# Node tiles in pairs, degrees per two groups, and gates applied in the tail of a graph and expert kernel

## The chip, the core and the metric

The kernel runs on one core of a Trainium2 chip, as one launch. The metric is the time on the device in microseconds. TensorE does the matrix products and transposes (PE in the profile, its weight loads PEld), VectorE (DVE) and ScalarE (ACT) the elementwise work, GpSimd (POOL) issues the indirect DMAs, which gather or scatter rows by a list of indices, and SyncE (SP) issues plain DMAs. Each engine works through its own instructions in order and waits on semaphores for the others.

## The reference

There are 12500 nodes with 256 features, 212500 edges sorted by their destination, and 64 experts with a hidden width of 512, of which each node uses two. Cut to what matters:

```python
def _forward(feats, ...):                      # feats is x, 12500 x 256
    deg_out = clip(segment_sum(ones, src), 1.0)
    deg_in = clip(segment_sum(ones, dst), 1.0)
    h = feats * rsqrt(deg_out)[:, None]
    m = segment_sum(h[src], dst) * rsqrt(deg_in)[:, None]
    x = m @ W_gc + b_gc + (feats @ W_res + b_res)
    core = moe(x)
    y = x + core
    mean, var = over the nodes, for each feature
    return (y - mean) * rsqrt(var + 1e-5) * gamma + beta

def moe(x):
    logits = x @ Wg + bg
    vals, idx = top_k(logits, 2)
    gates = softmax(vals)                      # of the two
    # expert e: gelu(x @ w1[e] + b1[e]) @ w2[e] + b2[e], for its first 1024 places
    return the sum over the two of gate * expert(x)

out = layernorm(x + _forward(x, ...))          # over the features
```

The softmax of two logits is a pair of gates: with d = second minus first, exp(d) is taken, the first gate is 1 / (1 + exp(d)) and the second exp(d) / (1 + exp(d)).

## The kernel before

Nodes are cut into 98 tiles of 128 (the last has 84), edges into 1664 columns of 128, and the columns into 208 groups of 8. Since the edges are sorted, the destinations of one group fall into a window of 128 nodes. The kernel has a setup (degrees by `src`, group windows, `h` scaled and written to `h_d`) and three stages.

**Node stage.** The loop over the groups calls `sums(g, n0, t0)`, and as soon as a node tile has all its edges, `node(t)`: once every two groups, now and then after three, twice after the last. In `sums`, each of the eight columns has an indirect DMA by POOL (L493) that gathers 128 rows of `h_d` into one of 16 tiles of `ring`, a one-hot matrix `o` made by VectorE (L499), and a matmul into `p` (L500), which has a last column of ones, so it counts the edges as well. `p` is copied by ScalarE to `s` (L503), transposed into `q` (L510), and VectorE adds it to the accumulator `acc2` in SBUF at the window's first node `n0` (L513). The counts go through `e` (L507), which splits them over the two node tiles that a window can touch, and a small matmul with `shift` (L511) into the last two columns of `q`, and are added to `deg_in` at a column `t0` read at run time (L515). `n0` and `t0` come in registers that VectorE loads for four groups at a time, eight values.

`node(t)` takes the reciprocal root of the in-degrees (`rsqrt`, L166 to L172: a root on ScalarE, four small operations and a reciprocal on VectorE), loads and scales the node's own features `xt` (L527), transposes them into `tp` (L530), copies them to `xT` (L532), and multiplies accumulator and features by the weights into `gp` (L535, L539; 256 features and 64 logits). VectorE scales and adds the bias: `y` (L540) and the logits `lg` (L549). Then come the two best experts (`top`, `i8`), the gates (exp on ScalarE L558, three VectorE operations to L561, kept in two extra columns of `y`), the store of `y` to `x2_d` by SP (L564), the rank of each token in its expert (`both` L572, matmuls into a part of `tp` L576 and L577, `ahead` L579, `total` L580, `junk` L584), the place code (L591 to L604), and four matmuls into the tables `tab` (L609 to L620). `tp` and `gp` have one buffer each, most other tiles of the node two. The exp and the root belong to different function tables, so ScalarE changes tables twice in a node.

**Experts.** After the tables are complete, the experts run in an order of their load. `gather` fetches rows of `x2_d` by POOL (L736), 258 floats a row: features and the two gate columns. `turn` transposes them (L752, copy L756) and picks the gate of each row (L758), `hidden` and `outputs` do the two matrix products (L770, L786). `outputs` adds the bias (L791), scales by the gate on ScalarE (L792), and scatters the rows to `z_d` by POOL (L793), which holds one row for each of a node's two choices. SP loads the weights.

**Tail.** For loads of eight node tiles, SP brings both rows of every node (`zt`, two buffers, L900), VectorE adds them to `acc2`, which by then holds `x`, in four additions (L904), TensorE transposes the sum (L915), and VectorE takes batchnorm statistics (L919). After the batchnorm numbers, a second loop applies them, adds the input and does the layernorm (L965 to L999).

The framework orders each engine's instructions so that node work is spread between the groups that follow; the source order above is not the engine's order.

Of the kernel before, what the change touches and what calls it, by code (L numbers as in the profile page):

```python
# [7 lines left out]
F32 = mybir.dt.float32  # L8
# [10 lines left out]
P = 128  # L19
# [3 lines left out]
E = 64  # L23
# [36 lines left out]


# [17 lines left out]
def gnn_moe_kernel(  # L79
# [25 lines left out]
    x2_d = dram.tile([N, D + 2], F32, name="x2_d")  # L105
# [53 lines left out]
    deg_in = const.tile([P, NT + 1], F32)  # L159
    V.memset(deg_in, 0.0)  # L160

# [29 lines left out]
    tables = route.tile([P, 2, 3, NSLOT], I32)  # L191
# [18 lines left out]
    til = edge.tile([P, NG, 2], F32)  # L210
    n0_row = edge.tile([1, 2, NG], I32)
# [4 lines left out]
    with ExitStack() as stack:  # L216
# [49 lines left out]
        def windows():  # L266
# [9 lines left out]
            V.tensor_copy(n0_row[:, 0], n0[:, 0])  # L276
            V.tensor_single_scalar(n0_row[:, 1], n0_row[:, 0], 7, op=ALU.arith_shift_right)
            V.tensor_copy(n0[:, 1], n0_row[:, 1])
# [34 lines left out]
            V.tensor_sub(til[:, :, 1], dig[:, 1], n0_b[:, 1])  # L313
            V.tensor_scalar(til[:, :, 0], til[:, :, 1], -1.0, 1.0, op0=ALU.mult, op1=ALU.add)
# [150 lines left out]
    with ExitStack() as stack:  # L465
# [21 lines left out]
        def sums(g, n0, t0):  # L487
# [14 lines left out]
            s = two.tile([P, D], F32, name="s")  # L502
            S.copy(s, p[:, :D])  # L503
            shift = two.tile([P, P], F32, name="shift")
            V.tensor_scalar(shift, lane, low[:, g : g + 1], None, op0=ALU.is_equal)
            e = two.tile([P, 2], F32, name="e")
            V.tensor_scalar(e, til[:, g], p[:, D:], None, op0=ALU.mult)  # L507
            q = ps2.tile([P, 2 * P + 2], F32, name="q")
            for h in range(2):
                T.transpose(q[:, h * P : (h + 1) * P], s[:, h * P : (h + 1) * P], ident)  # L510
            T.matmul(q[:, 2 * P :], shift, e, start=True, stop=True)  # L511
            m = acc2[:, :, bass.ds(n0, W)]
            V.tensor_add(m, q[:, : 2 * P].rearrange("p (h n) -> p h n", h=2), m)  # L513
            m = deg_in[:, bass.ds(t0, 2)]
            V.tensor_add(m, q[:, 2 * P :], m)  # L515

        def node(t):
            r = rows(t)
            y = two.tile([P, D + 2], F32, name="y")
            d_in = two.tile([P, 1], F32, name="d_in")  # L520
            V.tensor_scalar_max(d_in, deg_in[:, t : t + 1], 1.0)
            rsqrt(two, r_in[:, t : t + 1], d_in)
            root = two.tile([P, 1], F32, name="root")
            V.tensor_mul(root, d_in, r_in[:, t : t + 1])
            xt = two.tile([P, D], F32, name="xt", bufs=3)
            S.dma_start(xt[:r], x[t * P : t * P + r])
            S.activation(xt[:r], xt[:r], AF.Copy, scale=root[:r])  # L527
            tp = ps1.tile([P, 3, P], F32, name="tp")
            for k in range(2):
                T.transpose(tp[:, k, :r], xt[:r, k * P : (k + 1) * P], ident[:r, :r])  # L530
            xT = two.tile([P, 2, P], F32, name="xT")
            S.copy(xT[:, :, :r], tp[:, :2, :r])  # L532
            gp = ps1.tile([P, DL], F32, name="gp")
            for k in range(2):
                T.matmul(  # L535
                    gp[:r], acc2[:, k, t * P : t * P + r], wcat[:, k], start=k == 0, stop=False
                )
            for k in range(2):
                T.matmul(gp[:r], xT[:, k, :r], wcat[:, 2 + k], start=False, stop=k == 1)  # L539
            V.scalar_tensor_tensor(  # L540
                y[:r, :D], gp[:r, :D], r_in[:r, t : t + 1], bias[:r, :D],
                op0=ALU.mult, op1=ALU.add,
            )
            S.copy(
                acc2[:r, :, t * P : t * P + P],
                y[:r, :D].rearrange("p (h d) -> p h d", h=2),
            )
            lg = two.tile([P, E], F32, name="lg")
            V.scalar_tensor_tensor(  # L549
                lg[:r], gp[:r, D:], r_in[:r, t : t + 1], bias[:r, D:], op0=ALU.mult, op1=ALU.add  # L550
            )
            top = two.tile([P, 8], F32, name="top")
            V.max(top[:r], lg[:r])
            i8 = two.tile([P, 8], U32, name="i8")
            V.max_index(i8[:r], top[:r], lg[:r])
            e2 = two.tile([P, 2], F32, name="e2")
            V.tensor_sub(e2[:r, 0:1], top[:r, 1:2], top[:r, 0:1])
            S.activation(e2[:r, 0:1], e2[:r, 0:1], AF.Exp)  # L558
            V.tensor_scalar_add(e2[:r, 1:2], e2[:r, 0:1], 1.0)
            V.reciprocal(y[:r, D : D + 1], e2[:r, 1:2])  # L560
            V.scalar_tensor_tensor(  # L561
                y[:r, D + 1 :], e2[:r, 0:1], -1.0, y[:r, D : D + 1], op0=ALU.add, op1=ALU.mult
            )
            nc.sync.dma_start(x2_d[t * P : t * P + r], y[:r])  # L564
            ix = two.tile([P, 2], F32, name="ix")
            V.tensor_copy(ix[:r], i8[:r, 0:2])


            o1 = two.tile([P, E], BF16, name="o1")
            V.tensor_scalar(o1[:r], lane_b[:r, :E], ix[:r, 0:1], None, op0=ALU.is_equal)  # L570
            both = two.tile([P, E], BF16, name="both")
            V.scalar_tensor_tensor(  # L572
                both[:r], lane_b[:r, :E], ix[:r, 1:2], o1[:r], op0=ALU.is_equal, op1=ALU.add
            )
            pp = tp[:, 2].rearrange("p (k e) -> p k e", e=E)
            T.matmul(pp[:r, 0], before[:r, :r], both[:r], start=True, stop=True)  # L576
            T.matmul(pp[:, 1], ones_b[:r], both[:r], start=True, stop=True)  # L577
            ahead = two.tile([P, E], F32, name="ahead")
            V.tensor_add(ahead[:r], pp[:r, 0], total[:r])  # L579
            V.tensor_add(total, pp[:, 1], total)  # L580
            junk = two.tile([P, E], F32, name="junk")
            rk = two.tile([P, 2], F32, name="rk")
            for k in range(2):
                V.scalar_tensor_tensor(  # L584
                    junk[:r], lane[:r, :E], ix[:r, k : k + 1], ahead[:r],
                    op0=ALU.is_equal, op1=ALU.mult, accum_out=rk[:r, k : k + 1],
                )


            rk_i = two.tile([P, 2], I32, name="rk_i")  # L590
            V.tensor_copy(rk_i[:r], rk[:r])  # L591
            V.tensor_single_scalar(rk_i[:r], rk_i[:r], 7, op=ALU.arith_shift_right)
            blk = two.tile([P, 2], F32, name="blk")
            V.tensor_copy(blk[:r], rk_i[:r])
            lo = two.tile([P, 2], F32, name="lo")
            V.scalar_tensor_tensor(
                lo[:r], blk[:r], float(-P), rk[:r], op0=ALU.mult, op1=ALU.add
            )
# [28 lines left out]
        for g in range(NG):  # L627
# [19 lines left out]
            while done < ready:  # L647
                node(done)
                done += 1
# [391 lines left out]
```

## Time and profile before

| | us |
|---|---|
| median of 3 runs | 3864.94 |
| lowest, highest | 3864.89, 3868.7 |
| profiled execution, its time | 3846.16 |
| profiled execution, its span | 3844.4 |
| busy in the span: PE, PEld | 2581.5, 1896.3 |
| busy in the span: DVE, ACT, POOL | 1689.2, 1047.0, 2067.6 |
| first gather of the node stage, last | 247.9, 2687.4 |
| first expert gather | about 2729 |

The mean granted clock of TensorE is 0.806 of full speed. The profiled execution is one run and stands 18.8 us below the median; all durations of rows come from it. A line of the profile names source line, engine, operation, written and read tiles, and how often; "idle before" is how long the engine had waited, with the instruction that released it. A busy share over the whole span says little here, since the stages have different limits: the span is read by stage.

### The profile page before, as it was taken

To read this page: it belongs to the slowest core of one execution; us is meant where nothing else is said; L and a number is where in the kernel's file an instruction comes from. 1 tells how busy PE (TensorE), PEld (TensorE's weight loads), DVE (VectorE), ACT (ScalarE), POOL (GpSimd) and SP (SyncE) were. 2 spreads that over 40 slices of the span, in tenths; PEclk is the share of its full clock that TensorE was granted. 3 is DMA by queue.
4 is the path that set the end of the run, shared out by engine and by line. 5 is a ranking of instruction groups with operands and counts; after the bars stand their busy time and mean duration, and the time that the engine had idled before them with its cause. 6 is when DMAs were issued, how large, how long until landed. Compare 5 with 4: busy or idle time off the path is not lost. (4 is left out here: it accounts for less than half of the span.)

```text
span 3844.4 us, 40947 instructions
## 1 busy us (share of the span) xinstructions
PE 2581.5 (67%) x11395; PEld 1896.3 (49%) x11395; DVE 1689.2 (44%) x7659; ACT 1047.0 (27%) x2367; POOL 2067.6 (54%) x2165
## 2 busy tenths in 40 slices
PE   6725476565656656656665665665699999999630
PEld 5614354444444544444444444444477776777620
DVE  9953254443444444434444444444422222222497
ACT  8901021121112121212121122121233333333218
POOL 0046666666666666666666666666355555555100
PEclk8857788777778777777778677777899999999755
DMA  5085543333333333333333333333334444566666
GB/s 170 2 282 189 165 110 102 102 101 100 102 100 101 101 103 97 99 103 99 99 99 101 99 98 102 100 99 97 101 114 119 139 134 153 171 184 192 221 201 201
DMA packets 245787, 485.64 MB, mean 126 GB/s; under 512 B 45047, under 2 KB 157341, under 8 KB 237362
## 3 DMA queue, kind: packets, MB, share of 16 engines
q0 software_dynamic: 102640, 275.69, 25.6%
q1 hardware_dynamic: 128848, 194.48, 15.7%
q10 hardware_dynamic: 14066, 12.81, 1.1%
q8 instruction: 92, 1.51, 0.2%
q14 instruction: 141, 1.16, 0.1%
HBM read 393.01 MB, written 93.22 MB: 126 GB/s over the span
## 5 line engine op out<-in xcount | busy, mean ns | idle before, releaser
L493 POOL DMA_INDIRECT ring<-h_d,src_col x1664 | 1579.3, 949 | 873.4 <-issue 358.6
L500 PE MATMUL p<-ring,o 128*128 128x257 f32 x3328 | 994.8, 441 | 70.8 <-DMA z_d<-zero 51.0
L500 PEld LDWEIGHTS p<-ring,o 128*128 128x128 f32 x3328 | 702.3, 223 | 205.0 <-issue 90.6
L499 DVE TENSOR_SCALAR o<-lane,rel 128x128 f32<-128x128 f32 x1664 | 423.7, 301 | 193.3 <-remote 112.2
L786 PE MATMUL yp<-w,h 128*128 128x256 f32 (+3 forms) x1928 | 434.8, 381 | 4.1 <-ACT h L774 4.1
L770 PE MATMUL hp<-xT,w 128*128 128x384 f32 (+11 forms) x1328 | 400.2, 455 | 1.3 <-issue 1.3
L736 POOL DMA_INDIRECT xg<-x_d,tables x241 | 232.9, 967 | 305.6 <-PE xtp L752 208.1
L786 PEld LDWEIGHTS yp<-w,h 128*128 128x128 f32 (+3 forms) x1928 | 342.3, 182 | 70.0 <-issue 7.3
L535 PE MATMUL gp<-wcat,acc 128*128 128x320 f32 x392 | 185.5, 609 | 268.1 <-DVE acc L513 173.6
L513 DVE TENSOR_TENSOR acc<-q,acc 128x256 f32 x208 | 88.0, 423 | 564.2 <-remote 373.9
L503 ACT COPY s<-p 128x256 f32<-128x256 f32 x208 | 77.2, 371 | 921.7 <-remote 591.7
L793 POOL DMA_INDIRECT z_d<-yo,tables x241 | 238.0, 987 | 146.5 <-ACT yo L792 80.5
L770 PEld LDWEIGHTS hp<-xT,w 128*128 128x128 f32 x1328 | 248.3, 191 | 132.0 <-issue 59.2
L510 PE MATMUL q<-ident,s 128*128 128x128 f32 x416 | 103.7, 335 | 306.0 <-issue 185.0
L535 PEld LDWEIGHTS gp<-wcat,acc 128*128 128x128 f32 x392 | 94.0, 260 | 325.2 <-DVE acc L513 190.8
L510 PEld LDWEIGHTS q<-ident,s 128*128 128x128 f32 x416 | 62.6, 168 | 357.8 <-issue 215.5
L792 ACT ACTIVATE yo<-yo,gate 128x256 f32<-128x256 f32 (+3 forms) x241 | 122.3, 508 | 393.3 <-DVE yo L791 286.8
L791 DVE TENSOR_TENSOR yo<-yp,bb 128x256 f32<-128x256 f32 (+3 forms) x241 | 102.0, 423 | 284.1 <-PE yp L786 184.6
L774 ACT ACTIVATE h<-hp,w 128x384 f32<-128x384 f32 (+11 forms) x332 | 177.9, 544 | 170.4 <-PE hp L770 148.6
L539 PE MATMUL gp<-wcat,xT 128*128 128x320 f32 x392 | 152.9, 521 | 86.7 <-ACT xT L532 50.0
L756 DVE COPY xT<-xtp 128x768 f32<-128x768 f32 (+2 forms) x83 | 77.4, 932 | 299.8 <-PE xtp L752 299.5
L620 PE MATMUL tab<-at,vals 128*128 128x512 bf16 x392 | 144.4, 502 | 68.1 <-DVE at L609 28.8
(224 smaller groups left out, 3106.5 us busy)
## 6 DMA issues: line engine op xcount, KB each, us to landing
w<-in_wpack SPq DMA_DIRECT2D x64, 1026.0 KB
ring<-h_d,src_col POOLq DMA_INDIRECT x1664
z_d<-zero SPq DMA_DIRECT2D x98, 256.0 KB
zt<-z_d SPq DMA_DIRECT2D x24, 1024.0 KB
x_d<-y SPq DMA_DIRECT2D x97, 129.0 KB
xt<-in_x ACTq DMA_DIRECT2D x97, 128.0 KB
z<-in_x SPq DMA_DIRECT2D x12, 1024.0 KB
out<-z SPq DMA_DIRECT2D x12, 1024.0 KB
```

Of the source, the lines that this page charges most:

```text
L493: GP.indirect_dma_start(out=r[:, :D], out_offset=None, in_=h_d, in_offset=bass.IndirectOffsetOnAxis(ap=src_col[:, c : c + 1], axis=0),)
L499: V.tensor_scalar(o[:, j], lane, rel[:, c : c + 1], None, op0=ALU.is_equal)
L500: T.matmul(p, o[:, j], r, start=j == 0, stop=j == GR - 1)
L510: T.transpose(q[:, h * P : (h + 1) * P], s[:, h * P : (h + 1) * P], ident)
L535: T.matmul(gp[:r], acc2[:, k, t * P : t * P + r], wcat[:, k], start=k == 0, stop=False)
L539: T.matmul(gp[:r], xT[:, k, :r], wcat[:, 2 + k], start=False, stop=k == 1)
L620: T.matmul(tab[i], vals[:r, i], at[:r], start=t == 0 and k == 0, stop=t == NT - 1 and k == 1,)
L736: GP.indirect_dma_start(out=g, out_offset=None, in_=x2_d, in_offset=bass.IndirectOffsetOnAxis(ap=at[:, 0, k : k + 1], axis=0),)
L770: T.matmul(hp[:, :m], w1[:, c, j * P : (j + 1) * P], xT[:, c, :m], start=c == 0, stop=c == 1,)
L774: S.activation(h1[:, j, :m], hp[:, :m], AF.Gelu, bias=w[:, 2 * H + 4 * D + j : 2 * H + 4 * D + j + 1],)
L786: T.matmul(yp[:r], h1[:, j, k * P : k * P + r], w2[:, j], start=j == 0, stop=j == 3,)
L793: st = GP.indirect_dma_start(out=z_d, out_offset=bass.IndirectOffsetOnAxis(ap=at[:r, 1, k : k + 1], axis=0), in_=yo[:r], in_offset=None, b ...
```

## The change

Four things are done together.

1. `node(t)` becomes `nodes(t0, n)` and takes two tiles at once, except the last two tiles, which stay single. The small operations (degrees, roots, places) cover both tiles; transposes, matrix products and one-hot work are done for each tile in turn. `tp` has four parts instead of three, `gp` still one buffer. It is called after every second group only, if both tiles have their edges. The bias operation covers features and logits in one.
2. The degree counts of two groups are put together: `s` keeps the count column of both, `e` is made once for the pair, and two small matmuls sum into `q`. The columns of `deg_in` start at a fixed tile that the source knows, with a width of `TD` (4), instead of at a register. The register load brings four values instead of eight.
3. The gates are not made in the node stage: it keeps only the difference of the two best logits, in `less`. The two extra columns of `x2_d`, the third part of the tables, the gate pick in `turn` and the scaling in `outputs` are gone.
4. In the tail, the gates of all nodes are made at once from `less`. For each load, ScalarE scales the second row of each of the eight tiles by its gate, VectorE adds the first row times its gate to `acc2` tile by tile, and one addition adds the scaled second rows of all eight.

The core of the diff:

```diff
-        def sums(g, n0, t0):
+        def sums(g, n0):
...
-            s = two.tile([P, D], F32, name="s")
-            S.copy(s, p[:, :D])
-            shift = two.tile([P, P], F32, name="shift")
-            V.tensor_scalar(shift, lane, low[:, g : g + 1], None, op0=ALU.is_equal)
-            e = two.tile([P, 2], F32, name="e")
-            V.tensor_scalar(e, til[:, g], p[:, D:], None, op0=ALU.mult)
-            q = ps2.tile([P, 2 * P + 2], F32, name="q")
+            if g % 2 == 0:
+                pair["s"] = two.tile([P, 2, D1], F32, name="s")
+                pair["shift"] = two.tile([P, 2, P], F32, name="shift")
+            s, shift = pair["s"], pair["shift"]
+            S.copy(s[:, g % 2], p)
+            V.tensor_scalar(shift[:, g % 2], lane, low[:, g : g + 1], None, op0=ALU.is_equal)
+            q = ps2.tile([P, 2 * P + TD], F32, name="q")
             for h in range(2):
-                T.transpose(q[:, h * P : (h + 1) * P], s[:, h * P : (h + 1) * P], ident)
-            T.matmul(q[:, 2 * P :], shift, e, start=True, stop=True)
+                T.transpose(q[:, h * P : (h + 1) * P], s[:, g % 2, h * P : (h + 1) * P], ident)
             m = acc2[:, :, bass.ds(n0, W)]
+            if g % 2:
+                e = two.tile([P, 2, TD], F32, name="e")
+                V.tensor_tensor(
+                    e, til[:, :, g - 1 : g + 1].rearrange("p i g -> p g i"),
+                    s[:, :, D:].to_broadcast([P, 2, TD]), op=ALU.mult,
+                )
+                for i in range(2):
+                    T.matmul(q[:, 2 * P :], shift[:, i], e[:, i], start=i == 0, stop=i == 1)
             V.tensor_add(m, q[:, : 2 * P].rearrange("p (h n) -> p h n", h=2), m)
-            m = deg_in[:, bass.ds(t0, 2)]
-            V.tensor_add(m, q[:, 2 * P :], m)
+            if g % 2:
+                t = first_node(g - 1) // P
+                V.tensor_add(deg_in[:, t : t + TD], q[:, 2 * P :], deg_in[:, t : t + TD])
...
+        def nodes(t0, n):
+            r = rows(t0)
+            d_in = two.tile([P, 2], F32, name="d_in")
+            d_in = d_in[:, :n]
+            V.tensor_scalar_max(d_in, deg_in[:, t0 : t0 + n], 1.0)
+            rsqrt(two, r_in[:, t0 : t0 + n], d_in)
...
+            for i in range(n):
+                t = t0 + i
+                S.activation(xt[:r, i], xt[:r, i], AF.Copy, scale=root[:r, i : i + 1])
+                for k in range(2):
+                    T.transpose(tp[:, k, :r], xt[:r, i, k * P : (k + 1) * P], ident[:r, :r])
+                xT = two.tile([P, 2, P], F32, name="xT")
+                S.copy(xT[:, :, :r], tp[:, :2, :r])
+                gp = ps1.tile([P, DL], F32, name="gp")
...
+                V.scalar_tensor_tensor(
+                    y[:r, i], gp[:r], r_in[:r, t : t + 1], bias[:r], op0=ALU.mult, op1=ALU.add
+                )
+                V.max(top[:r, i], y[:r, i, D:])
+                V.max_index(i8[:r, i], top[:r, i], y[:r, i, D:])
...
+            V.tensor_sub(less[:r, t0 : t0 + n], top[:r, :n, 1], top[:r, :n, 0])
...
-            ready = first_node(g + 1) // P if g < NG - 1 else NT
-            while done < ready:
-                node(done)
-                done += 1
+            if g % 2:
+                ready = first_node(g + 1) // P if g < NG - 1 else NT
+                while done < NT:
+                    n = 2 if done < NT - 2 else 1
+                    if done + n > ready:
+                        break
+                    nodes(done, n)
+                    done += n
...
-        V.tensor_copy(slot[:, 2], second)
...
-            for k in range(n):
-                V.scalar_tensor_tensor(
-                    gate[:, k : k + 1], at[:, 2, k : k + 1], xg[k][:, D + 1 :],
-                    xg[k][:, D : D + 1], op0=ALU.mult, op1=ALU.add,
-                )
...
-                S.activation(yo[:r], yo[:r], AF.Copy, scale=gate[:r, k : k + 1])
...
+        gate = one.tile([P, 2, NT], F32)
+        S.activation(gate[:, 1], less, AF.Exp)
+        V.tensor_scalar_add(gate[:, 0], gate[:, 1], 1.0)
+        V.reciprocal(gate[:, 0], gate[:, 0])
+        V.tensor_mul(gate[:, 1], gate[:, 1], gate[:, 0])
...
-            for h in range(2):
-                y = half(h, t0, n, r)
-                for k in range(2):
-                    V.tensor_add(y, y, zt[:r, k, :n, h * P : (h + 1) * P])
+            for i in range(n):
+                t = t0 + i
+                S.activation(
+                    zt[:r, 1, i], zt[:r, 1, i], AF.Copy, scale=gate[:r, 1, t : t + 1]
+                )
+                y = acc2[:r, :, t * P : (t + 1) * P]
+                V.scalar_tensor_tensor(
+                    y, zt[:r, 0, i].rearrange("p (h d) -> p h d", h=2),
+                    gate[:r, 0, t : t + 1], y, op0=ALU.mult, op1=ALU.add,
+                )
+            y = acc2[:r, :, t0 * P : (t0 + n) * P].rearrange("p h (t d) -> p t h d", d=P)
+            V.tensor_add(y, y, zt[:r, 1, :n].rearrange("p t (h d) -> p t h d", h=2))
```

The window preparation makes `til` for `TD` tiles by comparing with the pair's first tile, a handful of small operations more.

## The prediction

> **What bounds the kernel now.** I read the page first (busy shares, the 40 slices, the costliest groups), then the busy time by stage, then the waits of each engine, then two timelines. The slices show three parts: a long middle where POOL has a 6 and TensorE a 5 or 6 (the node stage, 248 to 2690 us), the experts with TensorE at 9, and a tail where VectorE has a 9. By stage (columns: stretch and its length, busy us and instructions of PE, PEld, DVE, ACT, POOL, then granted clock, DMA share, GB/s):
>
> ```profile
> 1500.00:2000.00 500.00, 309.16 (x1168) 221.37 (x1168) 215.11 (x1278) 100.94 (x184) 320.14 (x338) 0.77 0.36 100
> 3000.00:3200.00 200.00, 200.00 (x880) 150.42 (x879) 51.98 (x138) 68.95 (x134) 110.24 (x113) 1.00 0.46 137
> 3640.00:3660.00 20.00, 10.07 (x43) 8.59 (x44) 18.91 (x22) 0.00 (x0) 0.00 (x0) 0.50 1.03 329
> ```
>
> No engine is full in the node stage, TensorE is full in the experts, VectorE in the tail. Each stage has to be argued from its own limit. For the node stage the waits of POOL, TensorE and VectorE (total us, times, longest; "remote" is the view's word for a release that came late, well after the recorded end of the instruction that gave it):
>
> ```profile
> POOL ring L493 <- issue: 358.6, 1081, 12.2
> POOL ring L493 <- remote: 266.6, 180, 4.7
> POOL ring L493 <- PE p L500: 186.4, 272, 3.0
> ...
> PE gp L535 <- DVE acc L513: 173.6, 32, 10.5
> PE gp L539 <- ACT xT L532: 50.0, 15, 9.5
> ...
> DVE acc L513 <- remote: 373.9, 55, 17.4
> ```
>
> And the timeline of POOL, then of TensorE, around one cycle (start, length, instruction, idle time before it):
>
> ```profile
> 1526.95 0.94 POOL L493 DMA_INDIRECT ring<-h_d,src_col  x1 [0.30 <-issue]
> 1528.19 0.94 POOL L493 DMA_INDIRECT ring<-h_d,src_col  x1 [0.30 <-issue]
> 1531.83 0.94 POOL L493 DMA_INDIRECT ring<-h_d,src_col  x1 [2.69 <-remote]
> ...
> 1523.19 1.11 PE L500 MATMUL p<-ring,o 128*128 128x257 f32 x4
> 1532.03 2.50 PE L535 MATMUL gp<-wcat,acc 128*128 128x320 f32 x4 [7.73 <-DVE acc L513]
> ```
>
> Unhindered, POOL issues a gather every 0.95 + 0.30 = 1.25 us; 1664 of them make 2080 us. The stage lasts 2440 us, so about 355 us are stalls of POOL with the ring of 16 tiles full. They come in turns of roughly one ring: POOL runs, TensorE meanwhile stands at a hand-off whose release comes late (the 7.73 us above), the ring fills, POOL stops, and then everything moves again. Taking 0.30 us of normal gap from each wait, the late releases are 267 - 180 x 0.3 = 213 us of the stalls and real waits for the p matmuls 186 - 272 x 0.3 = 105 us.
>
> Does a node tile cause a stall? The timeline answers: between two node tiles lie two groups of 8 gathers, now and then three. The 79 stretches of two groups take 23.2 to 23.6 us by where one cuts them, the 11 of three 34.5 to 37.0 us, 1.47 and 1.49 us a gather. An extra group without any node work costs its full 12 us, 2 of them stall. The pace goes by the gather and the ring, hardly by the node. This is the row that I rest on.
>
> **Node stage, the part that the change is about.** VectorE work removed, by the mean of each row: in a node the separate lg (274 ns, while y grows from 256 to 320 columns, about 67 ns), the three gate operations L559 to L561 (146 + 155 + 165), half of d_in, the five rsqrt steps and root (7 x 164 / 2), half of L557 and ix (163), half of rk_i to code (1222 / 2): near 2.0 us, 98 times, 198 us. In the groups, 104 of the 208 deg adds (152 ns) and of the e multiplies (249 ns): 42 us. ACT loses the exp of each node (203 ns) and all table changes, 89 + 90 loads of 1283 ns, so 250 us; its s copy grows by one column. TensorE's work stays: the degree matmuls are as many, four columns wide instead of two. On the queues, ACT's xt loads and SP's stores of x2 go from 98 to 50, each twice as large; VectorE's register loads bring four values instead of eight. POOL's own work is untouched. VectorE is 43% and ACT 20% busy here, so nearly all this 490 us lies beside idle time: cover is POOL's 1.25 us a gather. Without that cover VectorE's 240 us would be the most that could come back.
>
> What may count are hand-offs. Now every node has gp (L535) behind the acc add (L513), which stands on VectorE behind e and the degree matmul (L511) of the same group. Afterwards there is one such meeting in 32 gathers rather than two, and the even group's acc add no longer waits for a degree product. Of the named TensorE stops in this stage (173.6 and 50.0 above, 120.7 at q behind s, 43.0, 28.8, 25.8, 21.8: 464 us), gp behind acc has 37%; half of it gone is 19%. Put on all stalls that is -66 us, put on the 105 us of real p waits -20 us. Against it: inside a pair the second tile's tp and gp reuse the single buffers of the first, so new waits appear there, TensorE on ACT's xT copy and on VectorE's y; behind them stand the p matmuls, and for those POOL waits. From the three-group row I take -25 us, ends -150 us (nearly half of the stalls) and +90 us (the slower rival below).
>
> **End of the stage and experts.** From the last gather to the first expert gather 41 us pass, in which VectorE is busy 28 of 40 us. Nodes 96 and 97 are single there; without exp, table changes and the copy of the third table part I take -2 us (0 to -4). In the experts 241 gate operations (217 ns), 241 ACT scalings of yo (508 ns) and a third of the table copies go, all under a TensorE at 200 of 200 us; the scatter leaves half a microsecond sooner but nobody waits for it except at the very end, and the rows gathered shrink from 1032 to 1024 bytes. 0 us; without TensorE's cover it would be a gain, not a loss. Setup: the group windows gain a handful of small operations on one row and four compares, +1 us.
>
> **Tail.** VectorE is at 95% there. Its rows for this loop, and the two kinds of operation that replace the adds (from the final loop):
>
> ```profile
> L904 DVE TENSOR_TENSOR acc<-acc,zt 128x1024 f32<-128x1024 f32 x48 | 56.5, 1212 | 11.7 <-DMA zt<-z_d 11.7
> L919 DVE BATCH_NORM_STATS2 stat<-q 128x6 f32<-128x512 f32 x48 | 32.0, 690 | 3.1 <-PE q L915 1.6
> ...
> L977 DVE SCALAR_TENSOR_TENSOR z<-z,acc 128x256 f32<-128x256 f32 x97 | 36.8, 415 | 0.0
> L968 DVE TENSOR_TENSOR z<-z,ab 128x2048 f32<-128x2048 f32 x12 | 27.4, 2285 | 0.7 <-DMA z<-in_x 0.7
> ```
>
> Per load of eight tiles, four adds of 1024 become eight scaled adds of 256 and one add of 2048: the same elements, five more instructions. By the means that is 8 x 0.415 + 2.285 - 4 x 1.212 = +0.76 us, twelve times, +9 us. The timeline shows that a next instruction starts before the end of the one ahead (four adds in 4.61 us; scaled adds 0.345 us apart), which gives 2.76 + 2.21 - 4.61 = +0.36 us and +4 us. [...] The overlap in the timeline decides partly, as the bn operations stand between: I take +7 us. Added on ACT: eight scalings a load (508 ns as at L792), 4.1 us, idle engine, and the large add waits for all eight. Two buffers hold the loads, and the next one is asked for when the adds of the last but one are done; the scaled adds beside them take 2.8 us, so the wait is 0 if the second half lands 1.3 us ahead of VectorE's first scaled add, and up to that plus a small delay, 1.5 us a load (+18 us), if not. SP's next load stands behind that add; at a DMA share near 1.0, it would be late too. I take 0, and keep +18. Exp and the two small operations for the gates fall into VectorE's 11.7 us wait for the first load: 0.
>
> Sum: -25 - 2 + 0 + 1 + 7 = -19 us. The profiled execution took 3846.16 us (span 3844.4), 18.8 us below the median 3864.94 of the runs. I put the sum on the median: 3846 us.
>
> **The rivals.** *More hand-offs repaired (faster).* About a fifth of VectorE's instructions in the stage goes (by the counts above some 14 of 66 a node with its groups), and with fewer updates the releases might be less late. For it: nearly no late release stands in the experts, where fewer small instructions run. Against: the first three groups, before any node, are issued at full pace just because the ring is empty, and the fourth already stalls with no node done. If a third of the 355 us went: -118, with the rest about -112, 3753 us.
>
> *The pair stops TensorE longer (slower).* Place: the second tile's tp and gp directly behind the first's, and the acc add of the pair's second group directly ahead of gp. Row: after its 7.73 us stop, TensorE's four gp matmuls took 2.50 us, while the four of L539 take 1.24 us in the same cycle, and the stage's clock is 0.77. [...] It decides once the stops in a 32-gather turn last longer than the 16 tiles (20 us of POOL) that the ring holds.
>
> *Nothing in the node stage, and a late ACT in the tail.* Node 0, tail +7 and about +1.1 us of waiting a load (+13), the rest -1: 3884 us. For it: the three-group row, and a DMA share of 1.03.
>
> **How the numbers follow.** About 0.2% (8 us) is what a measurement can tell from no change. The forecast case (node 0 to -66, tail +4 to +12, the rest -1, hence 3802 to 3876 us) has 0.50, of which 0.31 faster, 0.12 same, 0.07 slower. The larger gain has 0.17, the longer stop 0.23, the tail case 0.10 (0.01 of it same). Faster 0.48, same 0.13, slower 0.39. The range runs from 3755, which leaves out about half of the large gain, to 3945, which leaves out somewhat over half of the stop case: near 0.79 inside.
>
> **What would show it.** Right: gathers still 1.25 us apart in runs, POOL stalls near 330 us, the acc wait ahead of gp smaller in times, the z loop 4 to 12 us longer. Wrong: stalls under 240 us (late releases depend on the work), or a larger gp or tp wait with a clock under 0.74, or ACT's scalings named ahead of the tail's large add.

## The result and the profile after

The changed kernel took 3923.42 us (median of 4 runs, 3910.27 to 3944.14) where the kernel before took 3866.82: 1.0151 times as long, interval 1.0106 to 1.0196. The forecast was 3846 us, a little faster. The result lies inside the stated range of 3755 to 3945 us, but on the other side of the kernel before. The profiled executions differ by 3908.3 - 3844.4 = 63.9 us. Read from the first or last instruction of each stage in the two timelines:

| stretch | before us | after us | difference |
|---|---|---|---|
| start to first gather | 247.9 | 248.0 | +0.1 |
| first to last gather of the node stage | 2439.5 | 2499.5 | +60.0 |
| last gather to first expert gather | 41.9 | 38.9 | -3.0 |
| first expert gather to the last expert matmul's end | 878.9 | 877.9 | -1.0 |
| from there to the last batchnorm statistics | 104.3 | 114.6 | +10.3 |
| from there to the end | 131.9 | 129.5 | -2.5 |

Nearly the whole loss is in the node stage, and ten microseconds are in the tail. The node stage by window, before and after (columns as in the prediction):

```profile
247.90:2687.40 2439.50, 1499.45 (x5636) 1079.67 (x5636) 1013.25 (x6079) 453.50 (x854) 1578.36 (x1664) 0.77 0.39 111
```

```profile
248.00:2747.50 2499.50, 1496.89 (x5598) 1062.77 (x5646) 905.99 (x4743) 193.93 (x491) 1583.59 (x1663) 0.76 0.36 108
```

TensorE (the first of the five busy times) works as long as before, 1497 us instead of 1499; the 60 us are time in which it stands. Shorter windows after, one in each of the three stages:

```profile
1500.00:2000.00 500.00, 305.85 (x1147) 218.45 (x1156) 186.89 (x969) 40.43 (x102) 317.24 (x334) 0.75 0.34 98
...
3200.00:3400.00 200.00, 200.00 (x805) 138.30 (x804) 40.70 (x71) 37.53 (x61) 108.40 (x111) 1.00 0.50 157
...
3700.00:3720.00 20.00, 10.33 (x47) 9.18 (x45) 19.87 (x35) 9.10 (x23) 0.00 (x0) 0.53 0.99 337
```

The work did go: from 1500 to 2000 us VectorE is busy 187 us instead of 215 and ScalarE 40 instead of 101. Yet POOL issues 334 gathers instead of 338. The waits of the whole span show what moved. First TensorE and POOL, then VectorE:

```profile
PE q L525 <- issue: 324.0, 49, 16.2
PE q L525 <- ACT s L521: 203.6, 36, 10.8
PE gp L570 <- ACT xT L562: 108.4, 20, 9.0
PE gp L570 <- issue: 105.6, 18, 10.7
...
POOL ring L508 <- PE p L515: 328.3, 357, 5.1
POOL ring L508 <- issue: 325.1, 990, 12.4
POOL ring L508 <- remote: 237.3, 237, 3.7
...
DVE at L633 <- PE q L525: 194.0, 27, 11.8
DVE at L633 <- remote: 125.9, 19, 9.6
```

Three things are to be seen. The stop of gp behind the acc add (173.6 us before) is all but gone (0.5 us), as the change should bring about. In its place the transposes into q stand behind the copy s, and gp behind xT. And VectorE has a wait that was hardly there (3 us before): ahead of `at` (L633).

"Issue" is the view's word where it names no release within the last microsecond. For q it hides the same wait: each of the 85 times that TensorE had stood ahead of q, q began 0.05 to 0.06 us after its s copy ended, and so it was in the 58 times before. So q stood behind s for 528 us after and for 306 us before, of which this row, the largest of TensorE's list before, is the greater part:

```profile
PE q L510 <- issue: 185.0, 35, 15.7
```

With POOL's normal gap of 0.30 us taken off, its waits for real p matmuls rose from 105 to 328 - 357 x 0.3 = 221 us, and the late releases fell from 213 to 166 us. So TensorE itself is later. Its stops by group between 500 and 2500 us, before and then after (the last column is idle time ahead of the group):

```profile
L535 PE MATMUL gp<-wcat,acc 128*128 128x320 f32 x328 | 157.9, 619 | 242.7 <-DVE acc L513 160.5 <-issue 69.8 <-DVE r_in L172 6.5
L539 PE MATMUL gp<-wcat,xT 128*128 128x320 f32 x332 | 131.2, 527 | 78.6 <-ACT xT L532 49.1 <-issue 23.0 <-ACT s L503 6.5
L510 PE MATMUL q<-ident,s 128*128 128x128 f32 x340 | 83.7, 331 | 195.5 <-ACT s L503 98.1 <-issue 97.2
```

```profile
L570 PE MATMUL gp<-wcat,xT 128*128 128x320 f32 x316 | 148.9, 611 | 201.0 <-issue 102.3 <-ACT xT L562 98.5
L565 PE MATMUL gp<-wcat,acc 128*128 128x320 f32 x317 | 140.2, 554 | 44.6 <-DVE y L571 26.9 <-issue 16.7 <-DVE o L514 0.7
L525 PE MATMUL q<-ident,s 128*128 128x128 f32 x332 | 90.0, 361 | 418.3 <-issue 246.4 <-ACT s L521 171.9
```

Gp behind acc lost 198 us, q gained 223 and gp behind xT 122.

### The profile page after: what moved, and what is told of

Same layout as the page of the kernel before. It is cut to its first block, busy times and chain, and to the rows that moved or that the text cites. A ratio compares the mean times of both kernels' runs of the same rounds, so it can differ in the third digit from the quotient of the medians.

```text
span 3908.3 us, 38148 instructions
## 1 busy us (share of the span) xinstructions
PE 2568.7 (66%) x11347; PEld 1875.2 (48%) x11395; DVE 1551.9 (40%) x6113; ACT 704.7 (18%) x1855; POOL 2072.9 (53%) x2165
## 5 line engine op out<-in xcount | busy, mean ns | idle before, releaser
L515 PE MATMUL p<-ring,o 128*128 128x257 f32 x3328 | 951.1, 432 | 58.7 <-DMA z_d<-zero 51.4
L514 DVE TENSOR_SCALAR o<-lane,rel 128x128 f32<-128x128 f32 x1664 | 402.9, 301 | 632.8 <-remote 360.1
L525 PE MATMUL q<-ident,s 128*128 128x128 f32 x416 | 112.7, 362 | 527.6 <-issue 324.0
L521 ACT COPY s<-p 128x257 f32<-128x257 f32 x208 | 77.8, 374 | 1551.6 <-remote 946.8
L570 PE MATMUL gp<-wcat,xT 128*128 128x320 f32 x392 | 178.4, 593 | 214.2 <-ACT xT L562 108.4
L789 PEld LDWEIGHTS hp<-xT,w 128*128 128x128 f32 x1328 | 248.2, 191 | 131.7 <-issue 58.9
L570 PEld LDWEIGHTS gp<-wcat,xT 128*128 128x128 f32 x392 | 95.9, 257 | 271.6 <-issue 140.8
L646 PE MATMUL tab<-at,vals 128*128 128x512 bf16 (+1 forms) x344 | 144.3, 519 | 117.7 <-DVE vals L641 33.8
L633 DVE TENSOR_SCALAR at<-slots,code 128x512 bf16<-128x512 f16 x196 | 67.2, 363 | 355.6 <-PE q L525 194.0
L565 PE MATMUL gp<-wcat,acc 128*128 128x320 f32 x392 | 170.4, 546 | 48.4 <-DVE y L571 27.5
```

What stands on the lines that cost most here:

```text
L514: V.tensor_scalar(o[:, j], lane, rel[:, c : c + 1], None, op0=ALU.is_equal)
L515: T.matmul(p, o[:, j], r, start=j == 0, stop=j == GR - 1)
L525: T.transpose(q[:, h * P : (h + 1) * P], s[:, g % 2, h * P : (h + 1) * P], ident)
L565: T.matmul(gp[:r], acc2[:, k, t * P : t * P + r], wcat[:, k], start=k == 0, stop=False,)
L646: T.matmul(tab[m], vals[:r, m], at[:r], start=t == 0 and k == 0, stop=t == NT - 1 and k == 1,)
L789: T.matmul(hp[:, :m], w1[:, c, j * P : (j + 1) * P], xT[:, c, :m], start=c == 0, stop=c == 1,)
```

## The experiments

Each ratio is the time divided by that of the kernel before, run on the same chip in the same set, with its 95% interval. The sets are not compared in microseconds: the kernel before had medians of 3848 to 3880 us in the first comparison and in four sets of experiments, and 3482.55 us in one set, of which below.

### The parts apart

The gates alone (a_gates, the gates-only kernel): `node` without exp and gate operations, tail of the changed kernel.

```diff
-            S.activation(e2[:r, 0:1], e2[:r, 0:1], AF.Exp)
-            V.tensor_scalar_add(e2[:r, 1:2], e2[:r, 0:1], 1.0)
-            V.reciprocal(y[:r, D : D + 1], e2[:r, 1:2])
...
+            V.tensor_sub(less[:r, t : t + 1], top[:r, 1:2], top[:r, 0:1])
```

> The kernel before with only the gates moved to the tail (no exp in the node stage, no gate columns, tail of the changed kernel); node tiles single, degrees per group as before. If the node stage is slowed by the pairing or by the shared degrees, the stage keeps its 2440 us from first to last gather or gains a little (0 to -25 us), and the tail costs what the changed kernel's did (+8 to +10 us), so 3855 to 3876 us in all. If the missing exp and table changes themselves upset the stage's rhythm (ScalarE then arrives early at s and waits), the stage is near 2500 us as in the changed kernel and the whole near 3920 us.

Measured 1.0100 (1.0082 to 1.0118). Removing work from ScalarE and VectorE lengthened the node stage, to 2486.6 us in the profiled execution (2439.5 before).

The changed kernel with single node tiles:

```diff
-                    n = 2 if done < NT - 2 else 1
+                    n = 1
```

> The changed kernel with node tiles taken one at a time (still only after every second group); shared degrees and gates in the tail stay. If the pairing is what costs the 60 us (two tiles' tp, gp and y chains one behind the other on single buffers), the stage returns to about 2440 us and the whole to about 3870 us, and TensorE's stops at gp behind xT fall from about 200 us per 2000 us back to under 100. If the shared degrees are to blame, it stays near 3920 us. If TensorE stops wherever the next hand-off is and the ring sets the pace, it differs from the changed kernel by under 15 us.

Measured 1.0069 (1.0051 to 1.0086): the pairing is part of the loss, not all of it. Between 500 and 2500 us gp behind xT stops for 18.9 us instead of 201.0, but q still for 376.5.

The changed kernel with degrees added per group at a register column, as before:

> The changed kernel with degrees added per group at a register column as before; pairs and gates in the tail stay. If the shared degrees cost the time (q transposes come earlier on TensorE behind the s copy, since the small degree matmul no longer stands with them), q behind s falls from about 418 us of TensorE stops per 2000 us to about 200 and the whole to about 3870 us. If the pairing costs it, it stays at 3910 to 3930 us.

Measured 1.0198 (1.0169 to 1.0227). The first theory is wrong: nothing came back, and q still stops for 376.1 us. The second, that the loss stays, holds or falls short: the interval overlaps those of the changed kernel (1.0151 at first, 1.0152 in a later set), so a further loss is not shown here. That the shared degrees gain is shown by the runs with them alone, below.

### The ring

```diff
-        for i in range(16):
+        for i in range(24):
```

> The kernel before with a ring of 24 instead of 16 gather tiles, nothing else changed. If each turn of the ring costs POOL one stall of fixed length (about 3.4 us in 16 gathers, since late releases only arrive once POOL stops), there are 69 turns instead of 104 and the stage loses about 118 us: 3750 us. If the stalls go by the gather whatever the depth (TensorE's own pace with its stops), the time stays within 20 us of 3867.

Measured 0.9998 (0.9989 to 1.0006). A stall of fixed length for each turn of the ring, as the prediction's turns "of roughly one ring" suggest, does not show: half as many tiles again change nothing, and the three longest of POOL's waits ahead of the ring (issue, remote and p) add up to 811 us (339.6 + 236.3 + 235.4) where they were 812 us with 16 tiles (358.6 + 266.6 + 186.4). So POOL's stalls go by the pace at which TensorE uses up the gathers.

### The missing work, or the order on TensorE

The framework's scheduler places node work between p matmuls anew when work is removed. The first test (a_keep) leaves the idle gate work in the gates-only kernel (its result is unused), which happens to give TensorE exactly the order of before:

```diff
+            S.activation(e2[:r, 0:1], less[:r, t : t + 1], AF.Exp)
             V.tensor_scalar_add(e2[:r, 1:2], e2[:r, 0:1], 1.0)
+            V.reciprocal(e2[:r, 2:3], e2[:r, 1:2])
...
```

> The gates-only kernel (gates in the tail) with the exp, its table changes and the three small gate operations left in each node tile, their result unused, so that TensorE's order of instructions in the node stage is the one of before. If the removal of that work itself upset the node stage (a new order on TensorE, another rhythm), the stage returns to 2440 us, and only the tail's and the experts' part remains: 1.002 to 1.003 of before. If something else in the gates' move is to blame (the rows of 1024 bytes in place of 1032, the smaller store), it stays near 1.010.

Measured 1.0006 (0.9994 to 1.0018): the loss is gone with the idle work back. To part the work from the order, the next two hold TensorE's 3464 node-stage instructions in a given order by issue-order edges and swap the orders of the two kernels:

```diff
+        order = "".join(c * int(n or 1) for n, c in _re.findall(r"(\d*)([a-i])", ORDER))
+        took = {a: iter(v) for a, v in kept.items()}
+        chain = [next(took[c]) for c in order]
+        for a, b in zip(chain, chain[1:]):
+            tc.add_manual_dep(
+                b, a.name,
+                mybir.DependencyInfo(mybir.DependencyClass.NoSync, mybir.DependencyReason.DATA),
+                reason="order",
+            )
```

> The gates-only kernel (exp, table changes and gate operations gone from the node stage, tail changed) with TensorE's instructions of the node stage held in exactly the order that they have in the kernel before, by issue-order edges. If the new order on TensorE made the gates-only kernel slow, this one is like the kernel that kept the idle gate work: 1.000 to 1.003 of before. If it is the missing work on ScalarE and VectorE itself (hand-offs that now come at other moments), it stays at 1.008 to 1.012.

> The converse: the kernel before, all its work kept, with TensorE's node stage held in the order that it has in the gates-only kernel. If the order costs the time, 1.006 to 1.010 of before, without any work added. If the work does, 0.999 to 1.002.

Measured 1.0016 (1.0007 to 1.0025) and 1.0000 (0.9991 to 1.0009), but in the set in which no release was late, where nothing could be told apart (see below). They were run again:

> The gates-only kernel with TensorE held in the order of before, once more, since the last chip showed no late releases at all and ran the node stage at POOL's pace in every kernel. On a chip whose releases come late: 1.000 to 1.003 if the new order on TensorE is what made the gates-only kernel slow, 1.008 to 1.012 if the missing work itself is. On a chip without late releases: 1.0016 as before, the tail alone.

> The kernel before with the gates-only kernel's order on TensorE, once more. With late releases: 1.006 to 1.010 if the order costs the time, 0.999 to 1.002 if the missing work does. Without: 1.000.

Now 0.9999 (0.9988 to 1.0009) and 1.0126 (1.0099 to 1.0153):

| | order of before | order of the gates-only kernel |
|---|---|---|
| all work of before | 1 | 1.0126 |
| gate work moved to the tail | 0.9999 | 1.0100 |

The order decides, the work does not. The kernel before, with not one instruction less or more, loses as much as the gates-only kernel when it gets that kernel's order on TensorE. Two limits: the edges hold TensorE alone, and the scheduler then places VectorE's instructions to suit (by the traces they stand on average some five places from where they stood before in before_ordA2, and some two in gates_ord2), so the finding is on TensorE's order with what follows from it. And the order of the changed kernel itself, with its pairs, was not held. The edges by themselves cost nothing that shows: gates_ord2 has them, a_keep has not, and both stand at 1.

### The pair's buffers

```diff
-                    at = two.tile([P, NSLOT], BF16, name="at")
+                    at = two.tile([P, NSLOT], BF16, name="at", bufs=4)
...
-                    vals = two.tile([P, 2, P], BF16, name="vals")
+                    vals = two.tile([P, 2, P], BF16, name="vals", bufs=4)
```

> The changed kernel with four buffers for at and vals instead of two, nothing else. The changed trace shows VectorE waiting 355 us ahead of at (L633), where before it waited 3 us ahead of L609: a pair makes four sets in a row, so the third waits until TensorE has used the first, and one-hot matrices for the next groups stand behind it. If this wait is the pairing's cost, 30 to 40 us come back: 1.005 to 1.008 of before. If TensorE only stops elsewhere, it stays within 10 us of the changed kernel, 1.013 to 1.017.

Measured 1.0080 (1.0056 to 1.0103) against 1.0151: about half of the changed kernel's loss is this wait, and in the trace no wait is left ahead of `at`. A pair makes four sets of `at` and `vals` in a row, two buffers hold two, and the third set waited for table matmuls that TensorE had queued; by the view, mostly behind a q that stood behind s (194.0 us above).

### Distance ahead of q

In TensorE's instruction order one can count how many p matmuls lie between the last p matmul of a group and the transposes of its sum into q; in this time ScalarE has to make s. The average is 1.91 in the kernel before, 1.52 in the gates-only kernel and 0.46 in the changed one. It does not rank the kernels by itself: single node tiles have 1.11 and lost less (1.0069) than the gates-only kernel, degrees per group have 0.91 and lost no less (1.0198) than the changed one. The next kernel (b_q4, average 4.12) is the one before, with a group's second half (s, q, the additions) put in the source after four p matmuls of the next group, and q held behind them:

```diff
+            if g + 1 < NG:
+                gathered(g + 1, 0, 4)
...
+            with tc.issue_after(held["mm"].ins):
+                for h in range(2):
+                    T.transpose(q[:, h * P : (h + 1) * P], s[:, h * P : (h + 1) * P], ident)
```

> The kernel before with the second half of a group (copy s, transposes into q, degree product, additions) put off on TensorE until four p matmuls of the next group have been issued; node tiles follow one group later. No work is added or removed. If slack between a hand-off's two TensorE ends decides the stage, the stops at q behind s (about 195 us in 2000) nearly go and 50 to 120 us are saved: 0.97 to 0.987. If TensorE stops at whatever hand-off comes next, the time stays within 10 us of before.

Measured 0.9956 (0.9941 to 0.9971), a gain, but less than I expected of it: between 500 and 2500 us the idle time ahead of q fell from 195.5 to 58.5 us, while that of gp behind xT rose from 78.6 to 151.4 and that of the table matmuls from 59.6 to 125.4. TensorE's stops mostly moved on.

```profile
L547 PE MATMUL gp<-wcat,xT 128*128 128x320 f32 x328 | 157.0, 619 | 151.4 <-ACT xT L540 102.4 <-issue 49.0
L518 PE MATMUL q<-ident,s 128*128 128x128 f32 x339 | 81.7, 313 | 58.5 <-ACT s L510 29.7 <-issue 28.7
```

The same edit, with the four buffers, on the changed kernel:

> The changed kernel with four buffers for at and vals, and with the copy s, the transposes into q and the additions of a group put off on TensorE until four p matmuls of the next group have been issued (no work added or removed). If the lost distance ahead of q (0.46 p matmuls on average in the changed kernel, 1.91 in the one before) is the rest of its loss, most of the node stage's loss comes back: 0.996 to 1.004 of before on a chip with late releases. If TensorE stops elsewhere for as long, 1.006 to 1.010 as with the buffers alone. Without late releases 1.001 to 1.003.

Measured 0.9909 (0.9895 to 0.9923). All of the loss came back and more: this version beats both kernels, by 0.9% against the one before. Its stops on TensorE:

```profile
L656 PE MATMUL tab<-at,vals 128*128 128x512 bf16 x328 | 127.0, 520 | 186.0 <-DVE at L643 83.7 <-DVE vals L651 30.8 <-issue 24.2
L533 PE MATMUL q<-ident,s 128*128 128x128 f32 x348 | 94.3, 340 | 146.2 <-issue 110.1 <-ACT s L528 28.5 <-ACT rsq_r L173 7.5
L570 PE MATMUL tp<-ident,xt 128*128 128x128 f32 x164 | 40.5, 337 | 142.3 <-ACT xt L568 99.1 <-issue 43.2
```

Q stops for 146 us instead of 418, tp and the table for more than in the changed kernel; POOL issues 348 gathers in 500 us instead of 334. The edit also lets the scheduler place everything else anew, so the gain belongs to the new order as a whole; that it is the distance ahead of q alone is not shown.

### Shared degrees alone, and both gains together

> Only the second part of the change: degrees of two groups added together at fixed columns, node tiles single and only after odd groups, gates as before. From the runs so far (gates-only 1.010, with shared degrees 1.007; pairs with per-group degrees 1.020, with shared ones 1.015) this part alone should gain: 0.994 to 0.998. If the gain only stood against the gates-only kernel's order, it is 1.000 to 1.008.

> Shared degrees alone, once more. With late releases: 0.994 to 0.998 if the part gains by itself as it did against the gates-only kernel; 1.000 to 1.008 if it too only brings another order on TensorE. Without: 1.000.

Measured 1.0003 (0.9994 to 1.0012) in the set without late releases and 0.9946 (0.9932 to 0.9960) in the later one: part 2 is a gain where releases are late. With q put off as well:

> Shared degrees alone (0.9946) with the same putting-off of q (0.9956 by itself on the kernel before). If distance between the two TensorE ends of a hand-off is what counts and adds up, 0.988 to 0.992 on a chip with late releases; if TensorE only stops at the next hand-off, 0.994 to 0.997. Without late releases 1.000.

Measured 0.9951 (0.9936 to 0.9965). The two gains of half a percent do not add up. The trace fits the rival that TensorE stops at the next hand-off: between 500 and 2500 us q stops for 62.6 us, but gp behind acc for 257.8, where shared degrees alone had 132.5.

### Breaks on POOL

> The kernel before with a small memset (128x128) on POOL after every fourth gather, so that POOL never issues more than four gathers back to back; nothing else. If TensorE's releases come late because POOL issues without a break, they come on time now, the late releases (remote) in POOL's and VectorE's waits fall by more than half, and the stage gets shorter by up to 60 us although POOL has some 0.1 us more work a gather. If the breaks don't matter, the stage keeps its time within 10 us, since POOL has slack; if POOL is the bound, it is 416 memsets longer, up to 80 us.

Measured 1.0080 (1.0060 to 1.0101). The memsets had drifted together, with none in 45 us of one timeline, so this run decides nothing. Held strictly after every fourth gather:

> The kernel before with a memset of 128x128 on POOL held strictly between every fourth gather and the next (the earlier such kernel let them drift together). 416 memsets of about 0.22 us and their gap are 110 us of POOL. If TensorE's releases come late because POOL issues gathers without a break, late releases go and the stalls (355 us) shrink by more than 110 us: at or below before. If breaks of this length do nothing to lateness and POOL's stalls only absorb them in part, +40 to +80 us.

Measured 1.0110 (1.0094 to 1.0125), in the set without late releases, so it could not answer either: whether breaks on POOL bring TensorE's releases on time stays open.

### A set without late releases

> The changed kernel itself, on the same chip as the three above. With late releases 1.011 to 1.020 as at first. Without them, TensorE never stops long, POOL sets the node stage in both kernels, and only the tail's 7 to 10 us less 3 us at the stage's end remain: 1.001 to 1.003. That would make the slowdown in the node stage a matter of late releases alone.

The changed kernel measured 1.0152 (1.0118 to 1.0186) here, as at first; this set had late releases. In the other set, that of gates_ord, before_ordA, deg_only and pace_f, the node stage took 2089 to 2090 us from first to last gather, and 2128 us with the memsets of pace_f, instead of about 2440. The kernel of before in the other order (before_ordA) there, by a window and by TensorE's longest wait (TensorE's instructions of the stage bear the lines of the helper that holds the order):

```profile
1500.00:2000.00 500.00, 394.53 (x1349) 240.75 (x1371) 253.95 (x1487) 116.50 (x215) 378.73 (x399) 0.86 0.41 118
...
PE p L527 <- DMA ring<-h_d,src_col: 390.8, 693, 3.0
```

and the same kernel in the later set (before_ordA2):

```profile
1500.00:2000.00 500.00, 303.69 (x1116) 216.05 (x1134) 210.57 (x1230) 96.20 (x176) 317.11 (x334) 0.78 0.35 98
...
PE q L532 <- issue: 232.6, 55, 12.3
PE gp L527 <- DVE acc L562: 212.6, 38, 9.7
```

In the first, POOL issues 399 gathers in 500 us, one every 1.25 us; no wait of any engine is marked remote, and TensorE waits for gathers, 3.0 us at the longest. Hand-offs are then hidden in either order (1.0000). In the second, stops stand at the hand-offs, in these two rows of up to 12.3 and 9.7 us.

That it is TensorE's releases that come late can be read from one hand-off in both directions. Between 500 and 2400 us, where ScalarE stood idle ahead of the copy s, s began more than 1 us after the last p matmul of its group had ended in 70 of 141 cases in the kernel before (12.5 us at the longest), in 77 of 157 in the changed kernel (16.4 us) and in 73 of 144 in before_ordA2. In the four kernels of the set without late releases it did so in none of 706, and 0.09 us was the longest. In the other direction nothing is late in either set: where TensorE stood ahead of q, q followed the end of s after 0.05 to 0.06 us.

The changed kernel itself was not run without late releases; gates_ord there shows what the move of the gates costs alone, 0.16%.

## Why the prediction was wrong

- **What bounds the stage.** Right that POOL would need 2080 us (2089 without late releases) and that the rest comes of late releases and TensorE's hand-offs. Wrong that the ring sets the pace: 24 tiles changed nothing (0.9998).
- **The step that failed: -25 us for the node stage, measured +60.** I counted hand-offs removed and took the rest of TensorE's order as given, although I had put into words that stops appear at whatever hand-off is next. The removed work changed the scheduler's order, and the order alone is worth 1.3% (before_ordA2, 1.0126, against gates_ord2, 0.9999). The row of the two- and three-group stretches, on which I rested, was read correctly, but it speaks only of one given order.
- **The row that was left out.** The 464 us of named stops leave out the rows marked "issue". With them q behind s stood for 306 us (185.0 + 120.7) and gp behind acc for 255 (81.1 + 173.6). These are two stops of like size; the change relieves one of them, and it is the other that grew.
- **What I costed at nothing.** The pair's four sets of at and vals on two buffers: I weighed only tp and gp. VectorE waited 355 us ahead of `at`, by the sum of that line's waits in the trace, and some 27 us (0.7%) came back with four buffers.
- **The slower rival.** Its sign and size were near (+90 us for the stage against +60), but that is luck in part, since its place was only partly right: gp behind xT did grow, by 122 us, but gp behind the first tile's y is 44.6 us in all, and the largest new stop is q behind s. The +90 us were my estimate, and no run shows them. What the runs show is slow work behind a stop: in the changed kernel four gp matmuls took 2.50 us after 7.37 us of stop, four others 1.24 us, which is 1.26 us less, and the mean clock fell from 0.806 to 0.798. It is not the length of the stop alone that decides: in the kernel before, between 400 and 2600 us, matmuls took over 1.5 times as long as the quickest fifth of their kind behind 75 of 86 stops of over 4 us, but also behind 28 of 46 of 2 to 4 us and behind 14 of 48 of 0.6 to 2 us. And slow work adds nothing to the loss: TensorE's busy time in the stage did not grow (1499.45 us before, 1496.89 after).
- **The signs.** Of those for being right, the gathers 1.25 us apart, the smaller acc wait and the longer tail came true, but POOL's stalls were near 420 us (2499.5 - 2080), not 330. Those for being wrong did not appear in a size that counts: gp stopped for less in all (261 us instead of 354) and so did tp, the clock stayed at 0.75 or above in the 500 us windows, and ScalarE's scalings are named ahead of the large add, but with 0.2 us. The way in which it went wrong was not among them.
- **Work removed.** The stage got no shorter for it, as argued, apart from the half per cent that the shared degrees gain. ScalarE's share is as reckoned (453.50 - 193.93 = 260 us, forecast 250). VectorE's was mis-sized as busy time: 1013.25 - 905.99 = 107 us less, where I had summed 240 from mean durations. As a sum it is right, the durations add up to 1496 us before and 1251 after; but neighbours overlap: in the timeline of before, two of L169 with a mean of 166 ns take 0.23 us together.
- **End of the stage, experts, setup.** -3.0 (forecast -2), -1.0 (0), +0.1 (+1).
- **Tail.** +10.3 us up to the last statistics, forecast +7. The scaled adds were mis-sized: 476 ns mean where I took 415, so the means give 8 x 0.476 + 2.288 - 4 x 1.212 = +1.25 us a load, and the overlap leaves 10.3 / 12 = 0.86. The fear for ScalarE's scalings was unfounded: the large add waited 0.2 us for them in all.

```profile
L929 DVE SCALAR_TENSOR_TENSOR acc<-zt,gate,acc 128x256 f32<-128x256 f32 x97 | 41.2, 476 | 9.4 <-DMA zt<-z_d 9.4
L934 DVE TENSOR_TENSOR acc<-acc,zt 128x2048 f32<-128x2048 f32 x12 | 27.5, 2288 | 0.7 <-ACT zt L925 0.2
```

The 2.5 us less after the statistics I had not foreseen. They come with the gates' move: 129.3 to 129.5 us in every run with the new tail, 131.7 to 132.3 in every one without. For 1.4 us of them the two timelines give the reason. Before, ScalarE loads the function table of the root only once the variance is there, and VectorE waits 1.7 us for the root; after, it has loaded it earlier, beside the last statistics, VectorE waits 0.3 us, and the first operation of the last loop follows those after 6.0 us instead of 7.4. The rest stays open. The two loads, before and after:

```profile
3713.59 1.28 ACT L166 ACT_TABLE_LOAD   x1 [104.37 <-DVE var L948]
```

```profile
3775.78 1.28 ACT L173 ACT_TABLE_LOAD   x1
```

## What to carry to other kernels

Where engines stop at hand-offs, an edit that only removes work can still cost time, because the scheduler orders the bottleneck engine anew (here 1.0100, and 0.9999 with the order held): compare that engine's order before and after, and part order from work by holding one order in both kernels. When tiles are paired, count the buffers of every tile that the pair makes in a row, not just the ones that the change names. Before a good idea is given up for its time, give it distance at its hand-offs: here the slower kernel became the fastest of those run with late releases (0.9909), with two more buffers for two tiles and four matmuls of delay. And when stops are listed, count the rows without a named release too; the instruction just ahead in the other engine's timeline tells what they waited for.

## What the hardware showed

TensorE's releases came late by microseconds (at the copy s by up to 12.5 us in the kernel before and 16.4 us in the changed one) in the first comparison and in four sets of experiments, and in no wait of the remaining set, with the same kernel: before_ordA took 3482.80 us in one and 3923.19 us in another. What sets this is not known. It is not the kernel, and a lasting property of one chip is not shown either: the set without late releases and the last set with them (at4_q4, deg_q4) both ran on a chip of the number 13. It is worth 12.6% in before_ordA (3923.19 / 3482.80), more than any edit here. Where releases are on time, the node stage runs at POOL's 1.25 us a gather (2089 to 2090 us for 1664) and order, shared degrees and gate work make no measurable difference (1.0000, 1.0003; 1.0016 with the cost of the gates' move).
